# Spreading the right-hand attention scores through a row in DRAM instead of by TensorE transposes

## The chip, the core and the metric

The kernel runs on one core of a Trainium2 chip. The time is the device time of one execution in microseconds (us). The core's engines work side by side, each through its own instructions in order: TensorE (PE, its weight loads shown apart as PEld), VectorE (DVE), ScalarE (ACT), GpSimd (POOL) and SyncE (SP), which issues the transfers between DRAM and the on-chip memory. An instruction waits for what it needs by semaphores. Matrix products land in eight PSUM banks; everything else is in SBUF, whose 128 partitions are the rows of each tile.

## What is computed

64 graphs of 256 nodes with 256 features, float32, and a 0/1 adjacency matrix for each. Two layers, each after a layer norm and a relu, each added to its input: a gated graph network of three rounds, then one graph attention layer.

```python
def _L0_gnn_ref(x, adj, weight, w_ih, w_hh, b_ih, b_hh):
    A = (adj != 0).astype(x.dtype)
    h = x
    for i in range(3):
        m = jnp.einsum('bnd,de->bne', h, weight[i])
        aggr = jnp.einsum('bst,bsd->btd', A, m)
        h = _gru_cell(aggr, h, w_ih, w_hh, b_ih, b_hh)
    return h

def _L1_gnn_ref(x, adj_matrix, W, a):
    h = jnp.einsum('bnd,od->bno', x, W)
    a_left, a_right = (a[0, :D], a[0, D:])
    e = (h @ a_left)[:, :, None] + (h @ a_right)[:, None, :]
    e = jnp.where(e > 0, e, 0.2 * e)
    e = jnp.where(adj_matrix == 0, -1e9, e)
    alpha = jax.nn.softmax(e, axis=-1)
    return jnp.einsum('bij,bjd->bid', alpha, h)

h = jnp.maximum(_layernorm(x), 0.0)
x = x + _L0_gnn_ref(h, adj, ...)
h = jnp.maximum(_layernorm(x), 0.0)
return x + _L1_gnn_ref(h, adj, ...)
```

The change concerns one line of the attention layer: in `e`, row i holds the left score of node i, one number for each partition, plus the right scores of all 256 nodes, which every partition needs along its row.

## The kernel before

The graphs go in 32 pairs of two (graph 0 and graph 1 of a pair). For each pair the kernel runs the layer norm ("in"), three rounds of the gated network, and the attention. The network's products are made of float32 values split into parts (`split`), so that a gate is a group of matmuls 512 wide: "top" groups (L456), a scaling of the bank on ACT ("scale", L470), then a "rest" group (L461). The letters are the gates: r, z, nh (the hidden side of n), ni (its input side), each for two halves of the features (r 0, r 1, ...). "prop" (L541) multiplies by the adjacency matrix, "turn" and "back" (L523, L584) transpose between the two layouts.

The attention of a pair, per graph g:

- "mid g": layer norm and relu of the residual (statistics on DVE, a power on POOL, relu on ACT at L496).
- "dot g" (L606): four products on DVE with the folded vectors W·a_left and W·a_right, each summed along the row into one column of a small tile: columns 12 and 13 are the left scores of the two halves of the nodes, 14 and 15 the right scores.
- "right g" (L617): two TensorE transposes, each with the column broadcast over 128 columns as the stationary operand, give a PSUM bank in which every partition holds all 256 right scores.
- "leaky g" (L621): two ACT passes read that bank, add the left score as the bias and apply the leaky relu.
- "mask g" (L624), "max g" (L626) on DVE, then "exps" on ACT (L633) for both graphs at once, with the load of another function table ahead of it.
- "p turn" (L648, PE), "p copy" (L652, ACT), "mix" (L657, PE), "mix copy" (L661, ACT), "project" (L666, PE), "out" (L671, DVE) and the store (L674, SP).

Nothing is issued in the order in which it is written. Every operation is an `Op` with an engine, a time in which it occupies the engine (`occ`), a time until its result is there (`lat`), and the buffers that it reads and writes. `Plan.run` then lays all of them out once, over the whole program: at each step it takes the operation that can start earliest, and among equals the one with the lowest priority number, which is worked back from due times and moved by the table `LEAD` ("right 0" is put back by 15000 ns there). Up to four pairs are open at once, so that between the steps of one pair's attention stand the gates of the next pair and the first steps of the one after it. The order so found is the order of the instructions on each engine; on the chip an engine keeps to it, also where an instruction has to wait. The result of an operation on the same engine counts as available after `occ`, on another engine after `lat`:

```python
for q in o.preds:
    t = max(t, q.start + q.occ if q.eng == e else q.end)
```

Buffers come from classes with a fixed number of slots: 28 "full" and 32 "round" tiles of 128 x 512 in SBUF, 12 "small" ones, and 8 "bank" tiles in PSUM. `pe`, `act`, `dve`, `pool` and `dma` make operations of the engine in their name.

Of the kernel before, what the change touches and what calls it, by code (L numbers as in the profile page):

```python
# [10 lines left out]
F32 = mybir.dt.float32  # L11
# [181 lines left out]
def tile_gated_gnn_then_gat(  # L193
# [35 lines left out]
    nc = tc.nc  # L229
    P = 128  # L230
    B, N, D = x.shape
    L = weight.shape[0]
    NB = N // P
# [5 lines left out]
    NPAIR = B // G  # L239
# [5 lines left out]
    plan = Plan(WINDOW, LEAD)  # L245
# [2 lines left out]
    plan.slot_class("x", [const.tile([P, GN], F32, name=f"x{i}") for i in range(2)])  # L248
    plan.slot_class("adj", [const.tile([P, GN], I32, name=f"adj{i}") for i in range(2)])
    plan.slot_class("small", [const.tile([P, 32], F32, name=f"small{i}") for i in range(12)])  # L250
    plan.slot_class("bank", [psum.tile([P, GN], F32, name=f"bank{i}") for i in range(8)])

    ALL = (0, 1)
    ONE = (0,)

    def parts(b):
        return b.t[:, :GN].rearrange("p (k d) -> p k d", k=2)
# [3 lines left out]
    def pe(name, n, fn, **kw):  # L261
        return plan.op(name, "PE", n, n + 220, fn, **kw)

    def act(name, n, fn, **kw):
        plan.op(name, "ACT", n, n + 170, fn, **kw)

    def dve(name, n, fn, **kw):
        plan.op(name, "DVE", n, n + 160, fn, **kw)

    def dve2(name, n, fn, **kw):  # L270
        plan.op(name, "DVE", n, n + 160, fn, port=True, **kw)

    def pool(name, n, fn, **kw):
        plan.op(name, "POOL", n, n + 200, fn, port=True, **kw)
# [5 lines left out]
    MM, TR, PROP, PASS = 432, 109, 120, 232  # L280
# [6 lines left out]
    ident = const.tile([P, P], F32, name="ident")  # L287
# [187 lines left out]
    def norm_relu(name, src, dst):  # L475

        sm = Buf("small")
        st = lambda k: sm.t[:, 6 * k : 6 * k + 6]
        mv = lambda: sm.t[:, 12:16].rearrange("p (k s) -> p k s", s=2)

        def stats():
            for nb in range(NB):
                nc.vector.bn_stats(st(nb), parts(src)[:, nb, :])
            for nb in range(NB):
                nc.vector.bn_aggr(mv()[:, nb, :], st(nb))

        dve(name + " stats", 900, stats, r=[(src, ALL)], w=[(sm, (0, 1))])
        dve(name + " eps", 70, lambda: nc.vector.tensor_scalar(sm.t[:, 16:18], mv()[:, :, 1], LN_EPS, None, op0=ALU.add),  # L488
            r=[(sm, (0, 1))], w=[(sm, (2,))])
        pool(name + " pow", 900, lambda: nc.gpsimd.tensor_tensor(sm.t[:, 16:18], sm.t[:, 16:18], nhalf, ALU.pow),  # L490
             r=[("nhalf", ONE)], w=[(sm, (2,))])
        dve2(name + " shift", 70, lambda: nc.vector.scalar_tensor_tensor(sm.t[:, 18:20], mv()[:, :, 0], -1.0, sm.t[:, 16:18],
                                                       op0=ALU.mult, op1=ALU.mult),
            r=[(sm, (0, 1, 2))], w=[(sm, (3,))])
        for nb in range(NB):
            act(name + " relu", 495, lambda nb=nb: nc.scalar.activation(  # L496
                parts(dst)[:, nb, :], parts(src)[:, nb, :], AF.Relu,
                bias=sm.t[:, 18 + nb : 19 + nb], scale=sm.t[:, 16 + nb : 17 + nb]),
                r=[(src, (nb,)), (sm, (2, 3))], w=[(dst, (nb,))])

    def pair(p):
# [7 lines left out]
        for g in range(G):  # L509
            dve2("A", 340, lambda g=g: nc.vector.tensor_scalar(A[g].t, ADJ[p][g].t, 0.0, None, op0=ALU.not_equal),  # L510
                r=[(ADJ[p][g], ALL)], w=[(A[g], ONE)])
# [3 lines left out]
                r=[(h[g], ALL), (hi[g], ONE)], w=[(lo[g], ONE)])  # L515
# [13 lines left out]
        for i in range(L):  # L529
# [22 lines left out]
            for db in range(DB):  # L552
# [4 lines left out]
                    r=[(pr, ONE), ("b_rz", ONE)], w=[(r_, ONE)])  # L557
# [3 lines left out]
                    r=[(ph, ONE), (r_, ONE)], w=[(u, ONE)])  # L561
# [3 lines left out]
                    r=[("vec", ONE)], w=[(u, ONE)])  # L565
# [3 lines left out]
                    r=[(pz, ONE), ("b_rz", ONE)], w=[(z_, ONE)])  # L569
# [8 lines left out]
            for g in range(G):  # L578
# [11 lines left out]
                else:  # L590
                    act(f"hi {g}", A512 + 10, lambda b=hi[g], pt=pt: nc.scalar.copy(b.t, pt.t), r=[(pt, ONE)], w=[(hi[g], ONE)])
                    dve(f"lo {g}", V512, lambda b=hi[g], c=lo[g], pt=pt: nc.vector.tensor_sub(c.t, pt.t, b.t.bitcast(F32)),  # L592
                        r=[(pt, ONE), (hi[g], ONE)], w=[(lo[g], ONE)])
# [5 lines left out]
        for g in range(G):  # L599
            pool("fill", 520, lambda b=pm_[g]: nc.gpsimd.memset(b.t, NEG_INF), w=[(pm_[g], ALL)])  # L600
            norm_relu(f"mid {g}", XR[g], hb[g])
            sm = sms[g]
            for nb in range(NB):
                for n in range(2):
                    c = 12 + n * NB + nb
                    dve2(f"dot {g}", 425, lambda g=g, nb=nb, n=n, c=c, sm=sm: nc.vector.scalar_tensor_tensor(  # L606
                        parts(sc[g])[:, nb, :], parts(hb[g])[:, nb, :], 1.0, va[:, n, :], op0=ALU.mult, op1=ALU.mult,
                        accum_out=sm.t[:, c : c + 1]),
                        r=[(hb[g], (nb,)), ("va", ONE)], w=[(sm, (c,)), (sc[g], (nb,))])


            pR = Buf("bank")

            def right(sm=sm, pR=pR):
                for nb in range(NB):
                    c = 12 + NB + nb
                    nc.tensor.transpose(pR.t[:, ts(nb, P)], sm.t[:, c : c + 1].to_broadcast([P, P]), ident)  # L617

            pe(f"right {g}", 2 * TR, right, r=[(sm, (14, 15))], w=[(pR, ONE)])
            for nb in range(NB):  # L620
                act(f"leaky {g}", 365, lambda b=sc[g], nb=nb, pR=pR, sm=sm: nc.scalar.activation(  # L621
                    parts(b)[:, nb, :], pR.t[:, :N], AF.Prelu, bias=sm.t[:, 12 + nb : 13 + nb], alpha=LEAKY_SLOPE),
                    r=[(pR, ONE), (sm, (12 + nb,))], w=[(sc[g], (nb,))])
            dve2(f"mask {g}", 660, lambda g=g: nc.vector.copy_predicated(pm_[g].t, A[g].t.bitcast(I32), sc[g].t),  # L624
                r=[(A[g], ONE), (sc[g], ALL)], w=[(pm_[g], ALL)])
            dve(f"max {g}", 610, lambda b=pm_[g], sm=sm: nc.vector.tensor_reduce(sm.t[:, 0:NB], parts(b), AX.X, ALU.max, negate=True),  # L626
                r=[(pm_[g], ALL)], w=[(sm, ONE)])

        def exps():
            for g in range(G):  # L630
# [6 lines left out]
                w=[(b, ALL) for b in pm_] + [(s, (1,)) for s in sms])  # L637

        for g in range(G):
            sm = sms[g]  # L640
            dve("recip", 70, lambda sm=sm: nc.vector.reciprocal(sm.t[:, 8 : 8 + NB], sm.t[:, 4 : 4 + NB]),
                r=[(sm, (1,))], w=[(sm, (2,))])
# [35 lines left out]
    for p in range(NPAIR):  # L678
        if p > 0:
            plan.pair = p  # L680
            load_pair(p)
        pair(p)
# [28 lines left out]
```

## Time and profile before

| | |
|---|---|
| median of 3 runs | 2248.85 us (2248.42 to 2250.21) |
| profiled execution, time | 2247.52 us |
| profiled execution, span from first to last instruction | 2245.7 us |
| PE busy in the stretch 115 to 1100 us | 982.58 of 985 us |
| "right", L617 matmul records | 128, mean 279 ns |
| "leaky", L621 | 128, mean 472 ns |
| DRAM traffic | 71.75 MB, mean 32 GB/s, all queues |

The profile is one execution, recorded instruction by instruction. A group of instructions has a count, a busy time and a mean length; records of matmuls overlap, since TensorE begins one before the last has left, so the time that a matmul takes from the engine is read from one start to the next. The waits name, for an engine and a line, the instruction that ended an idle time. The chain of waits goes back from the last instruction to what released it. The answer on a tile's transfers gives the time from a transfer's issue to its landing.

### The profile page before, as it was taken

To read this page: it belongs to the slowest core of one execution; us is meant where nothing else is said; L and a number is where in the kernel's file an instruction comes from. 1 tells how busy PE (TensorE), PEld (TensorE's weight loads), DVE (VectorE), ACT (ScalarE), POOL (GpSimd) and SP (SyncE) were. 2 spreads that over 40 slices of the span, in tenths; PEclk is the share of its full clock that TensorE was granted. 3 is DMA by queue.
4 is the path that set the end of the run, shared out by engine and by line. 5 is a ranking of instruction groups with operands and counts; after the bars stand their busy time and mean duration, and the time that the engine had idled before them with its cause. 6 is when DMAs were issued, how large, how long until landed. Compare 5 with 4: busy or idle time off the path is not lost.

```text
span 2245.7 us, 31163 instructions
## 1 busy us (share of the span) xinstructions
PE 2213.2 (99%) x10977; PEld 1822.5 (81%) x10977; DVE 1825.2 (81%) x4084; ACT 1662.8 (74%) x3069; POOL 140.6 (6%) x198
## 2 busy tenths in 40 slices
PE   8999999999999999999999999999999999999997
PEld 6788888888888888888888888888888888888875
DVE  7878877879878888778788778797787887787974
ACT  8677777777777777777777777777777777777764
POOL 1000000000000000000000000000000000000000
PEclk9999999999999999999999999999999999999998
DMA  3000111001111001110011110011110011100000
GB/s 103 20 20 29 38 38 38 20 20 38 38 39 34 24 20 38 38 38 29 15 33 39 38 38 20 20 39 38 38 34 24 20 38 38 38 29 15 15 19 28
DMA packets 72541, 71.75 MB, mean 32 GB/s; under 512 B 4272, under 2 KB 72384, under 8 KB 72384
## 3 DMA queue, kind: packets, MB, share of 16 engines
q1 hardware_dynamic: 72352, 69.75, 10.2%
q8 instruction: 86, 1.41, 0.3%
q14 instruction: 71, 0.58, 0.1%
q10 hardware_dynamic: 32, 0.01, 0.0%
HBM read 52.96 MB, written 16.78 MB: 31 GB/s over the span
## 4 chain that ended last, share of the span: by engine, by line
PE 70%; DVE 19%; ACT 8%; issue 3%; DMA 0%; ACTq 0%; POOL 0%; DVEq 0%; POOLq 0%
PE bank L456 32%; PE bank L461 16%; PE bank L541 5%; PE bank L657 5%; PE bank L666 5%; DVE round L442 4%; PE bank L584 3%; DVE round L443 3%; ACT full L496 2%; DVE full L314 2%; DVE full L574 2%; DVE full L573 2%; ACT bank L470 2%; DVE round L592 2%; PE bank L648 1%
## 5 line engine op out<-in xcount | busy, mean ns | idle before, releaser
L456 PE MATMUL bank<-round,fac_hh 128*128 128x512 f32 x2304 | 635.0, 402 | 0.5 <-DVE round L442 0.5
L456 PE MATMUL bank<-round,fac 128*128 128x512 f32 x2304 | 600.3, 395 | 0.0
L456 PEld LDWEIGHTS bank<-round,fac 128*128 128x128 f32 x2304 | 433.2, 188 | 103.4
L456 PEld LDWEIGHTS bank<-round,fac_hh 128*128 128x128 f32 x2304 | 410.7, 189 | 74.3 <-DVE round L442 1.0
L461 PE MATMUL bank<-round,fac_hh 128*128 128x512 f32 x1152 | 383.0, 413 | 0.7 <-ACT bank L470 0.7
L470 ACT ACTIVATE bank<-bank 128x512 f32<-128x512 f32 x576 | 327.5, 579 | 62.5 <-PE bank L456 62.3
L461 PE MATMUL bank<-round,fac 128*128 128x512 f32 x1152 | 355.5, 398 | 1.0 <-ACT bank L470 1.0
L441 ACT CAST round<-full 128x512 fp32r<-128x512 f32 x384 | 238.3, 621 | 156.9 <-DVE full L314 156.9
L442 DVE TENSOR_TENSOR round<-full,full 128x512 fp32r<-128x512 f32 x384 | 259.5, 689 | 8.7
L573 DVE TENSOR_TENSOR full<-full,full 128x512 f32<-128x512 f32 x192 | 129.3, 686 | 168.6 <-ACT full L567 168.5
L461 PEld LDWEIGHTS bank<-round,fac 128*128 128x128 f32 x1152 | 210.2, 188 | 61.9 <-ACT bank L470 16.4
L443 DVE SCALAR_TENSOR_TENSOR round<-round,full 128x512 fp32r<-128x512 f32 x384 | 255.5, 686 | 3.4
L461 PEld LDWEIGHTS bank<-round,fac_hh 128*128 128x128 f32 x1152 | 202.0, 189 | 48.5 <-ACT bank L470 16.4
L541 PEld LDWEIGHTS bank<-round,round 128*128 128x128 f32 x1536 | 204.7, 189 | 14.2 <-DVE round L592 0.9
L541 PE MATMUL bank<-round,round 128*128 128x256 f32 x1536 | 214.9, 285 | 0.7 <-DVE round L592 0.7
L572 DVE TENSOR_TENSOR full<-full,full 128x512 f32<-128x512 f32 x192 | 128.3, 681 | 106.4 <-ACT full L564 106.4
L490 POOL TENSOR_TENSOR small<-small,nhalf 128x2 f32<-128x2 f32 x128 | 106.1, 829 | 1477.6 <-DVE small L488 1476.8
L567 ACT ACTIVATE full<-bank,b_rz 128x512 f32<-128x512 f32 x192 | 132.2, 689 | 71.4 <-PE bank L461 71.1
L545 ACT COPY full<-bank 128x512 f32<-128x512 f32 x192 | 112.9, 588 | 88.2 <-PE bank L541 88.2
L314 DVE TENSOR_SCALAR full<-full 128x512 int32<-128x512 int32 (+1 forms) x400 | 161.7, 418 | 6.5 <-ACT full L545 5.0
L563 DVE TENSOR_TENSOR full<-full,bank 128x512 f32<-128x512 f32 x192 | 131.9, 687 | 40.8 <-PE bank L461 31.4
L556 ACT ACTIVATE full<-bank,b_rz 128x512 f32<-128x512 f32 x192 | 131.2, 684 | 40.4 <-PE bank L461 40.1
(74 smaller groups left out, 2723.0 us busy)
## 6 DMA issues: line engine op xcount, KB each, us to landing
x<-in_x_dram SPq DMA_DIRECT2D x64, 256.0 KB, 2.7
adj<-in_adj_dram SPq DMA_DIRECT2D x64, 256.0 KB, 2.7
full<-in_x_dram SPq DMA_DIRECT2D x64, 256.0 KB, 3.1
out_dram<-full SPq DMA_DIRECT2D x64, 256.0 KB, 2.2
full<-in_L_gnn_w_ih_dram SPq DMA_DIRECT2D x3, 256.0 KB, 4.2
full<-in_L_gnn_weight_dram SPq DMA_DIRECT2D x3, 256.0 KB, 4.6
full<-in_L_gnn_w_hh_dram SPq DMA_DIRECT2D x3, 256.0 KB, 5.3
full<-in_L_gnn_W_dram SPq DMA_DIRECT2D x1, 256.0 KB
```

The costliest lines, as they stand in the source:

```text
L314: dve2(name, 60 + n * 0.54, lambda: nc.vector.tensor_scalar(dst().bitcast(I32), src().bitcast(I32), CUT, None, op0=ALU.bitwise_and), r=r, w=w)
L441: act(name + " 0", C512, lambda: nc.scalar.copy(v0.t, t.t), r=[(t, ONE)], w=[(v0, ONE)])
L442: dve2(name + " 1", V512, lambda: nc.vector.tensor_sub(v1.t, v.t, t.t), r=[(v, ALL), (t, ONE)], w=[(v1, ONE)])
L443: dve2(name + " d", V512, lambda: nc.vector.scalar_tensor_tensor(vd.t, v1.t.bitcast(F32), -SPLIT, t.t, op0=ALU.mult, op1=ALU.add), r=[(v1, ...
L456: nc.tensor.matmul(bank.t, f(m, j, kb), b.t, start=(first and n == 0), stop=True, skip_group_check=True)
L461: nc.tensor.matmul(bank.t, f(m, 2, kb), s[kb][2].t, start=False, stop=True, skip_group_check=True)
L470: act(name + " scale", A512, lambda: nc.scalar.activation(bank.t, bank.t, AF.Identity, bias=bias, scale=1.0 + C), r=[("vec", ONE)], w=[(ba ...
L541: nc.tensor.matmul(pa.t[:, ts(g, N)], parts(b)[:, sb, ts(db, P)], parts(A[g])[:, sb, :], start=(n == 0), stop=(n == len(terms) - 1))
L556: act(f"r {db}", 575, lambda b=r_, k=pr, db=db: nc.scalar.activation(b.t, k.t, AF.Sigmoid, bias=b_rz[:, db : db + 1]), r=[(pr, ONE), ("b_r ...
L563: dve(f"u add {db}", V512, lambda u=u, k=pn: nc.vector.tensor_add(u.t, u.t, k.t), r=[(pn, ONE)], w=[(u, ONE)])
L567: act(f"z {db}", 575, lambda b=z_, k=pz, db=db: nc.scalar.activation(b.t, k.t, AF.Sigmoid, bias=b_rz[:, DB + db : DB + db + 1]), r=[(pz, O ...
L573: dve2(f"d mul {db}", V512, lambda d=d, b=z_: nc.vector.tensor_mul(d.t, d.t, b.t), r=[(z_, ONE)], w=[(d, ALL)])
```

## The change

For all pairs but the last, the two transposes of "right" are replaced by two transfers on SP. "line" writes the two columns of right scores (128 partitions x 2 numbers of 4 bytes) into a row of 256 numbers in DRAM. "right" reads this row back with all 128 partitions as its destination, 1 KB into each, into a "full" tile. "leaky" reads that tile in place of the PSUM bank. There are four rows in DRAM for this, and their slots are handed out by the planner like those of the other classes. The last pair keeps the transposes. The planner's table `LEAD` and all other operations are as they were; the planner lays out the whole order anew.

```diff
+    dram = ctx.enter_context(tc.tile_pool(name="dram", bufs=1, space=bass.MemoryType.DRAM))
+    plan.slot_class("line", [dram.tile([1, N], F32, name=f"line{i}") for i in range(4)])
     plan.slot_class("bank", [psum.tile([P, GN], F32, name=f"bank{i}") for i in range(8)])
...
-            pR = Buf("bank")
-
-            def right(sm=sm, pR=pR):
-                for nb in range(NB):
-                    c = 12 + NB + nb
-                    nc.tensor.transpose(pR.t[:, ts(nb, P)], sm.t[:, c : c + 1].to_broadcast([P, P]), ident)
-
-            pe(f"right {g}", 2 * TR, right, r=[(sm, (14, 15))], w=[(pR, ONE)])
+            if p < NPAIR - 1:
+                line, pR = Buf("line"), Buf("full")
+                plan.op(f"line {g}", "SP", 150, 2800, lambda line=line, sm=sm: nc.sync.dma_start(
+                    line.t.rearrange("o (nb q) -> (o q) nb", q=P), sm.t[:, 12 + NB : 12 + 2 * NB]),
+                    r=[(sm, (14, 15))], w=[(line, ONE)])
+                plan.op(f"right {g}", "SP", 150, 2600, lambda line=line, pR=pR: nc.sync.dma_start(
+                    pR.t[:, :N], line.t.to_broadcast([P, N])), r=[(line, ONE)], w=[(pR, ONE)])
+            else:
+                pR = Buf("bank")
+
+                def right(sm=sm, pR=pR):
+                    for nb in range(NB):
+                        c = 12 + NB + nb
+                        nc.tensor.transpose(pR.t[:, ts(nb, P)], sm.t[:, c : c + 1].to_broadcast([P, P]), ident)
+
+                pe(f"right {g}", 2 * TR, right, r=[(sm, (14, 15))], w=[(pR, ONE)])
             for nb in range(NB):
                 act(f"leaky {g}", 365, lambda b=sc[g], nb=nb, pR=pR, sm=sm: nc.scalar.activation(
                     parts(b)[:, nb, :], pR.t[:, :N], AF.Prelu, bias=sm.t[:, 12 + nb : 13 + nb], alpha=LEAKY_SLOPE),
```

## The prediction

> **What bounds the kernel now.** I read the head of the page and its chain, then the busy time by stretches, then the waits, then the groups of the removed operation and the timelines around it, last the answers on the transfers.
>
> ```profile
> span 2245.7 us, 31163 instructions
> PE 2213.2 (99%) x10977; PEld 1822.5 (81%) x10977; DVE 1825.2 (81%) x4084; ACT 1662.8 (74%) x3069; POOL 140.6 (6%) x198
> ...
> PE 70%; DVE 19%; ACT 8%; issue 3%; DMA 0%; ACTq 0%; POOL 0%; DVEq 0%; POOLq 0%
> ```
>
> ```profile
> 1100.00:2150.00 1050.00, 1047.82 (x5237) 867.44 (x5236) 860.76 (x1921) 785.91 (x1447) 64.89 (x88) 1.00 0.10 31
> 2150.00:2245.70 95.70, 76.37 (x346) 60.44 (x344) 58.16 (x138) 52.97 (x99) 2.76 (x4) 0.91 0.05 17
> ```
>
> TensorE is the bound and is full: in the 1050 us of the first stretch it is idle for 2.2. (Columns: window, length, busy PE, PEld, DVE, ACT, POOL, clock, DMA share, GB/s.) So a slot taken from PE's queue shortens the run by that slot, and a wait put in front of PE lengthens it by the wait: there is nothing to absorb it. The waits show how little the operation costs now:
>
> ```profile
> ACT full L652 <- PE bank L648: 29.7, 33, 1.0
> ...
> PE bank L648 <- ACT full L633: 3.0, 1, 3.0
> ...
> ACT full L621 <- PE bank L617: 2.9, 11, 0.9
> ```
>
> ACT's leaky pass (L621) hardly waits for the transposes (L617), and PE waits for the exponentials (L633) only in the last pair. The removed transposes and their slot, on PE's timeline in a middle pair (start, length):
>
> ```profile
> 813.22 1.09 PE L456 MATMUL bank<-round,fac 128*128 128x512 f32 x4
> 814.15 0.62 PE L461 MATMUL bank<-round,fac 128*128 128x512 f32 x2
> 814.61 0.38 PE L617 MATMUL bank<-ident,small 128*128 128x128 f32 x2
> 814.83 0.60 PE L523 MATMUL bank<-ident,full 128*128 128x128 f32 x4
> ...
> 829.70 0.38 PE L617 MATMUL bank<-ident,small 128*128 128x128 f32 x2
> 829.84 1.18 PE L456 MATMUL bank<-round,fac_hh 128*128 128x512 f32 x4
> 830.85 1.10 PE L456 MATMUL bank<-round,fac 128*128 128x512 f32 x4
> ```
>
> A record lasts 0.27 us or more, but records overlap; start to next start counts. The first pair of transposes holds PE for 0.22. The second holds it for 0.14, and the four matmuls behind it take 1.01 instead of the usual 0.93: 0.22 as well.
>
> **What the Trainium skill says.** "DMA: Bandwidth & Descriptors", section "Anatomy of one DMA", puts about 2 us of fixed cost on a transfer, most of it the receipt from the written memory. The trace agrees: a 256 KB store lands 2.2 us after its issue, a 256 KB load of x after 2.7. The same page, "Rules for kernel authors", says that a non-contiguous last dimension becomes one descriptor per element, and that a DMA that reads what another wrote has to wait for the other's completion. No run here shows the first yet. By it the column becomes 256 pieces of 4 bytes, and by the second the two latencies add. "TensorE: Matmul & The Clock Gate", table at the top, calls the queues of ScalarE and VectorE strict FIFOs: an ACT instruction that waits holds all behind it. The waits and timelines agree.
>
> **The change, part by part.**
> *Removed.* 31 pairs x 2 graphs = 62 couples of transposes, 62 x 0.22 = 13.6 us of PE. Nothing else falls away. The bank that they filled comes free, but PE's 2.2 idle us in the stretch above leave nothing for a further bank to win.
>
> *Added on the queues.* 62 writes and 62 broadcast reads on SP. SP's loads of the next pair stand ahead of them, the stores of this pair follow some 20 us later, so nothing urgent is behind them. Traffic grows by 62 x 128 KB = 8 MB on 71.75, at a DMA share of 0.10. Both at nothing; if the queues were crowded the two latencies below would grow.
>
> *The new wait.* Leaky now needs two transfers in series after the last dot product.
>
> ```profile
> L674 SPq DMA_DIRECT2D out_dram<-full x64: 383/384/387, 164.5 to 2242.6; - x64
> ...
> DMA to landing us min/median/max: 2.1/2.2/4.6
> ```
>
> The answer for x is 2.5/2.7/4.6. Write: a 256 KB store is 256 packets of 1 KB, the column 256 pieces of 4 bytes, so I take the store's 2.2. Queue 1 of the page gives a packet 10.2% x 16 x 2245.7 / 72352 = 51 ns, so the store's 16 packets per engine are 0.8 of that. If a small piece cost nothing the write would take 1.4; if a piece under 512 B cost twice a packet (the page's table of specifications speaks of read-modify-write there; no trace here shows it) 3.0. Read: x's 2.7 less half its packets, 8 x 51 ns = 0.4, gives 2.3. Low bound 2.1, as no load here lands sooner; high 3.1, if 128 reads of one row get in each other's way. Hand-offs: DVE to SP 0.03 (846.37 + 0.87 against SP's issue at 847.27), and 0.05 to 0.1 for each of the other two. Sum 4.7, from 3.7 to 6.3.
>
> *What covers it.* The planner gives its ops on one engine a start after the other's issue, not after its landing; so to it "right" starts 150 ns after "line", and it puts leaky about 2.75 us behind the dot products. I take the cover from the order in which the changed kernel issues its work, with durations of the trace of before. Zero is the issue of r 1's rest on PE. PE then has 2 + 1 + 2 + 4 + 1 couples of wide matmuls (r 1 rest, nh 1 rest, ni 1 top, z 0 top, ni 1 rest) at 0.93 for two couples: 4.66. The turn of the next pair adds 0.60 (L523 above), ACT copies it (0.47 to its next instruction): leaky of graph 1 has its turn at 5.8. Against that the last dot product: r 0's sigmoid starts 0.2 to 0.5 after zero (two relu passes stand ahead), 0.69; DVE's multiply 0.60, dot product 0.43: 1.9 to 2.2, and I take 2.4 for the other dot products in DVE's queue. Cover 5.8 - 2.4 = 3.4. ACT waits 4.7 - 3.4 = 1.3. Graph 0's row is fetched meanwhile and comes as its leaky has its turn, so it adds nothing.
>
> *Who waits behind it.* On ACT, from the first leaky to the exponentials, in the new order, by the spacings of ACT's timeline: leaky 2 x 0.37, tanh 0.61, three copies or scales of a bank in 0.47 to 0.52 (prop 1, prop 0, z 1's scale) and nh 0's scale 0.52, sigmoid 0.58, leaky 2 x 0.37, three casts (h0, g0, g1) 0.53: 6.3. Exponentials 3.4 with their table load (833.02 to 836.40), hand-off 0.1: 9.8. PE from the same moment: what it still has ahead of the turn of the exponentials, counted from zero, is 4.66 + 0.44 (turn) + 2 x 0.96 (prop) + z 0 rest 0.93 + z 1 top 1.86 + six groups of four (nh 0 top, r 1, z 1 rest, r 0 twice, ni 0) 5.58 = 15.4, less 5.8: 9.6. So the new order holds no slack there (the old one put the turn 0.6 after the exponentials' end, 836.40 to 836.97): even without ACT's wait PE would be 0.15 late. With it, PE stands 1.3 + 0.15 = 1.45 per pair, a good half of it already at nh 0's top, which needs h0's cast from ACT. DVE is held too (mask 1 needs leaky) but nothing of it reaches PE sooner.
>
> *Sum.* 31 x 1.45 = 45, less 13.6: +31 us. Profiled execution: span 2245.7, time 2247.52; 2247.5 + 31 = 2279. The median shown is 1.3 above that execution: 2280. The last pair keeps its transposes; the tail is costed at nothing, 2 us either way.
>
> **Rivals.**
> *A. The small pieces are dear.* Write 3.0, read 3.1, L = 6.3: wait per pair 6.3 - 3.4 + 0.15 = 3.05; 94.6 - 13.6 = +81, 2330. For it: the page counts 4272 packets under 512 B but prices none of them, so nothing here shows what a 4-byte write costs. Against: 256 pieces are only 16 per engine.
> *B. The cover holds, and the change is faster.* Place: leaky of graph 1 on ACT. It decides at a round trip of 3.4 - 0.15 + 13.6 / 31 = 3.7 us; at 3.2 or less the whole slot is won, 2248.85 - 13.6 = 2235. For it: ACT is idle for 26% and ahead of PE elsewhere (it waits 82.4 us for L456 in all). Against: 3.7 is my low bound for two latencies in series.
> *C. Wait and slot cancel,* within 4.5 us: a round trip of 3.6 to 3.8, or DVE's dot products done half a us earlier together with a cheap write. 2249.
>
> **How the numbers follow.** Forecast 0.70 (round trip 4.0 to 5.6, wait 0.75 to 2.3: +10 to +58, 2259 to 2307); A 0.17; B 0.08; C 0.05. About 0.2% is what a measurement of this kernel can tell from no change. Most of B is faster: 0.06; same 0.05; slower 0.89. The range reaches from the cheap end of the forecast, 2256, into the first half of A, 2322.
>
> **What would show it.** In the changed profile: L617's transposes at 4 (now 128); a new wait of ACT's leaky for the landed row, 31 times or more, 1 to 1.6 us each; new waits of PE for ACT's cast and for the exponentials, 1.45 us per pair, and PE at 97% (2200 of 2277); landings of about 2.2 and 2.3. Wrong if leaky finds its row landed (B), if the two landings add to more than 5.5 (A), or if PE stands at another line, which would mean that the new order, not the transfers, costs the time.

## The result, and the profile after

The changed kernel takes 2806.07 us in the median of 4 runs (2803.83 to 2813.82), the kernel before 2249.24 beside it: a ratio of 1.2482, 95% interval 1.2456 to 1.2507. The direction was as forecast, the size was not: +557 us against +31.

The page of the changed kernel: span, busy times, and the two new transfers (KB each, median us from issue to landing).

```profile
span 2805.9 us, 30945 instructions
...
PE 2312.1 (82%) x10853; PEld 1886.9 (67%) x10853; DVE 1832.8 (65%) x4084; ACT 1677.4 (60%) x3069; POOL 136.8 (5%) x198
...
full<-line SPq DMA_DIRECT2D x62, 128.0 KB, 4.8
line<-small SPq DMA_DIRECT2D x62, 1.0 KB, 9.1
```

PE has lost its fill: idle for 2805.9 - 2312.1 = 493.8 us against 32.5 before, which is +461. And it is busy for 98.9 us more although 124 matmuls are gone. The two make up the whole difference of the spans, 560. The write of the column, the smallest transfer of the kernel (1 KB), takes the longest to land.

Its waits (engine and line, what it waited for: us in total, times, longest):

```profile
ACT full L632 <- DMA full<-line: 527.5, 62, 15.6
DVE full L635 <- ACT full L632: 512.4, 61, 15.3
...
PE bank L458 <- ACT round L443: 297.9, 30, 15.2
...
PE bank L463 <- ACT bank L472: 159.1, 38, 13.0
...
PE bank L659 <- ACT full L644: 3.0, 1, 3.0
```

Most of the links are the predicted ones: leaky (now L632) waits for the row, DVE's mask for leaky, PE for the cast (L443) that stands behind leaky on ACT. PE's second wait is for a scale of a bank (L472) that stands behind the other graph's leaky, and not for the exponentials (L644), as predicted: for these PE waits once, 3.0 us, as before. And ACT waits at both graphs, 62 times, and 8.5 us each. The timeline of one pair, first SP, then ACT, then PE (start, length, in brackets the idle time before):

```profile
995.28 0.37 SPq L617 DMA_DIRECT2D line<-small  x1
1003.55 0.34 SPq L620 DMA_DIRECT2D full<-line  x1
1003.99 0.39 SPq L617 DMA_DIRECT2D line<-small  x1
1014.97 0.33 SPq L620 DMA_DIRECT2D full<-line  x1
```

```profile
998.00 0.59 ACT L529 COPY full<-bank 128x512 f32<-128x512 f32 x1 [0.31 <-PE bank L525]
1008.62 0.51 ACT L632 ACTIVATE full<-full,small 128x256 f32<-128x256 f32 x1 [10.04 <-DMA full<-line]
...
1019.78 0.91 ACT L632 ACTIVATE full<-full,small 128x256 f32<-128x256 f32 x2 [7.58 <-DMA full<-line]
```

```profile
1001.56 1.10 PE L458 MATMUL bank<-round,fac 128*128 128x512 f32 x4
1012.25 3.78 PE L458 MATMUL bank<-round,fac_hh 128*128 128x512 f32 x8 [9.59 <-ACT round L443]
1021.73 1.22 PE L463 MATMUL bank<-round,fac_hh 128*128 128x512 f32 x2 [5.70 <-ACT bank L472]
```

Graph 1's column is written for 8.2 us before SP can issue the read. The last dot product of graph 0 ended at 998.59, but its write is issued at 1003.99: it stands behind that read in SP's queue, and the read behind the landing. So the two round trips run one after the other. After the first wait PE's eight matmuls take 3.78 us. A like group of eight took 2.02 before:

```profile
819.96 2.02 PE L456 MATMUL bank<-round,fac_hh 128*128 128x512 f32 x8
```

Where the write's time goes shows when the same pair is cut into stretches, here the busy share of the 16 DMA engines in 40 slices of 0.25 us between 995 and 1005 and the packets in it:

```profile
DMA  0000230000000000000000000000000000000000
...
DMA packets 272, 0.00 MB, mean 0 GB/s; under 512 B 272, under 2 KB 272, under 8 KB 272
```

and the stretches themselves (window, length, busy PE, PEld, DVE, ACT, POOL with counts, granted clock, DMA share, GB/s):

```profile
997.00:1003.00 6.00, 5.66 (x35) 4.64 (x33) 3.33 (x10) 1.28 (x3) 0.00 (x0) 1.00 0.00 0
1003.00:1005.00 2.00, 0.00 (x0) 0.00 (x0) 0.00 (x0) 0.00 (x0) 0.00 (x0) 0.95 0.00 0
1005.00:1007.00 2.00, 0.00 (x0) 0.00 (x0) 0.00 (x0) 0.00 (x0) 0.00 (x0) 0.50 0.06 23
1012.25:1016.03 3.78, 3.78 (x8) 2.47 (x8) 0.82 (x2) 0.00 (x0) 0.00 (x0) 0.50 0.17 1
```

The pieces are sent within 0.5 us, from 996.0 to 996.5. For the next 7 us no packet moves, and the write has still not landed. So the cost is no work of the DMA engines; it lies between the last packet and the landing. The Trainium skill ("DMA: Bandwidth & Descriptors", section "Anatomy of one DMA") says that the receipt of the target memory is most of a DMA's fixed cost of about 2 us; the section is written for transfers that GpSimd issues, and these are issued by SP. The place agrees; the size here, 8.2 us for this write, is four times that. The 272 packets are the 256 pieces of the forecast and 16 more. The last two stretches show the second loss: with PE idle its granted clock falls to 0.50, and it is still 0.50 during the eight matmuls after the wait. Over the whole run it is 0.898 against 0.996.

Landings of the writes come in two sizes. A pair's first write (graph 1) takes 8.2 us in the median, its second (graph 0), issued just behind the read of the first, 10.4. In this pair the second write is issued at 1003.99, but its packets move only between 1007 and 1008.5, among and after those of the read, which had itself been late.

### The profile page after: what moved, and what is told of

The parts are those of the page before. It is cut to its first block, busy times and chain, and to the rows that moved or that the text cites. A ratio compares the mean times of both kernels' runs of the same rounds, so it can differ in the third digit from the quotient of the medians.

```text
span 2805.9 us, 30945 instructions
## 1 busy us (share of the span) xinstructions
PE 2312.1 (82%) x10853; PEld 1886.9 (67%) x10853; DVE 1832.8 (65%) x4084; ACT 1677.4 (60%) x3069; POOL 136.8 (5%) x198
## 5 line engine op out<-in xcount | busy, mean ns | idle before, releaser
L458 PE MATMUL bank<-round,fac_hh 128*128 128x512 f32 x2304 | 698.7, 434 | 298.5 <-ACT round L443 297.9
L458 PEld LDWEIGHTS bank<-round,fac_hh 128*128 128x128 f32 x2304 | 461.8, 209 | 405.4 <-ACT round L443 311.2
L458 PE MATMUL bank<-round,fac 128*128 128x512 f32 x2304 | 617.6, 402 | 0.0
L463 PE MATMUL bank<-round,fac_hh 128*128 128x512 f32 x1152 | 397.4, 427 | 156.6 <-ACT bank L472 156.6
L458 PEld LDWEIGHTS bank<-round,fac 128*128 128x128 f32 x2304 | 443.0, 193 | 104.6
L472 ACT ACTIVATE bank<-bank 128x512 f32<-128x512 f32 x576 | 332.7, 583 | 126.5 <-PE bank L458 123.8
L635 DVE COPY_PREDICATED full<-round,full 128x512 f32<-128x512 int32 x64 | 46.7, 730 | 512.5 <-ACT full L632 512.4
L632 ACT ACTIVATE full<-full,small 128x256 f32<-128x256 f32 x124 | 59.4, 503 | 527.5 <-DMA full<-line 527.5
L463 PE MATMUL bank<-round,fac 128*128 128x512 f32 x1152 | 372.6, 410 | 2.5 <-ACT bank L472 2.5
L463 PEld LDWEIGHTS bank<-round,fac_hh 128*128 128x128 f32 x1152 | 206.0, 195 | 213.7 <-ACT bank L472 184.8
L443 ACT CAST round<-full 128x512 fp32r<-128x512 f32 x384 | 234.5, 620 | 109.9 <-DVE full L316 109.9
L463 PEld LDWEIGHTS bank<-round,fac 128*128 128x128 f32 x1152 | 221.3, 195 | 60.2 <-ACT bank L472 11.5
L575 DVE TENSOR_TENSOR full<-full,full 128x512 f32<-128x512 f32 x192 | 132.3, 689 | 136.4 <-ACT full L569 136.3
L566 ACT ACTIVATE full<-full,vec 128x512 f32<-128x512 f32 x192 | 138.9, 723 | 98.0 <-DVE full L565 94.2
L492 POOL TENSOR_TENSOR small<-small,nhalf 128x2 f32<-128x2 f32 x128 | 97.0, 758 | 1626.5 <-DVE small L490 1530.4
L594 DVE TENSOR_TENSOR round<-bank,round 128x512 fp32r<-128x512 f32 x128 | 87.9, 688 | 117.7 <-ACT round L593 115.5
```

What stands on the lines that cost most here:

```text
L443: act(name + " 0", C512, lambda: nc.scalar.copy(v0.t, t.t), r=[(t, ONE)], w=[(v0, ONE)])
L458: nc.tensor.matmul(bank.t, f(m, j, kb), b.t, start=(first and n == 0), stop=True, skip_group_check=True)
L463: nc.tensor.matmul(bank.t, f(m, 2, kb), s[kb][2].t, start=False, stop=True, skip_group_check=True)
L472: act(name + " scale", A512, lambda: nc.scalar.activation(bank.t, bank.t, AF.Identity, bias=bias, scale=1.0 + C), r=[("vec", ONE)], w=[(ba ...
L566: act(f"tanh {db}", 615, lambda u=u, en=en: nc.scalar.activation(u.t, u.t, AF.Tanh, bias=b_i[:, en : en + 1]), r=[("vec", ONE)], w=[(u, ONE)])
L575: dve2(f"d mul {db}", V512, lambda d=d, b=z_: nc.vector.tensor_mul(d.t, d.t, b.t), r=[(z_, ONE)], w=[(d, ALL)])
```

## The experiments

Theory 1: the loss is the wait for the round trip, and nothing else. Its first rival, theory 2: the new order or the small writes' traffic costs by itself. Inside theory 1 it was open what makes a write of 1 KB take 9.1 us: a cost of each piece (1a), a fixed one (1b), or pieces that meet at one place in DRAM (1c). Times are medians; those without an interval are of a single run. Before stood at 2248.0 to 2248.6 in these runs.

### The wait taken away: no_wait and own_tile

```diff
-                    parts(b)[:, nb, :], pR.t[:, :N], AF.Prelu, bias=...
+                    parts(b)[:, nb, :], va[:, 1, :], AF.Prelu, bias=...
```

> Leaky reads a constant tile (va) of the same size in place of the fetched row; both transfers are still issued, nothing on ACT waits for them, and the issue order is that of the changed kernel. Left out: the right scores in leaky. Theory 1 (the whole loss is the wait for the round trip): before less the removed slots, plus the 0.15 us per pair by which the new order alone is late: 2249 - 13.6 + 4.6 = 2240, between 2233 and 2250; PE idle under 40 us, clock near 0.996. Theory 2 (the new issue order or the traffic of small writes costs by itself): above 2300.

Measured: 2502.05 us, ratio 1.1134 (1.1115 to 1.1153). By the number alone this is theory 2. The waits tell another story:

```profile
DVE full L316 <- DMA full<-line: 192.4, 30, 10.7
...
ACT full L663 <- DMA full<-line: 87.3, 25, 4.9
```

The fetched tile is handed out again once leaky is done, as the planner sees it. With leaky no longer waiting, the next users of that tile wait for the landing instead. The experiment had moved the wait, not removed it. So once more, with leaky reading the constant as before and a tile of its own for the row:

```diff
+    sink = [const.tile([P, N], F32, name=f"sink{i}") for i in range(1)]
-                    pR.t[:, :N], line.t.to_broadcast([P, N])), r=[(line, ONE)], w=[(pR, ONE)])
+                    sink[k], line.t.to_broadcast([P, N])), r=[(line, ONE)], w=[(pR, ONE)])
```

> As in no_wait, leaky reads a constant tile, but now the fetched row also goes to a tile of its own that nothing reads and no other operation reuses, so that no engine but SP can wait for a transfer. Left out: the right scores. Theory 1 (the loss is waits for the transfers, in no_wait by the operations that reuse the tile as a buffer): 2233 to 2250, no wait of ACT, DVE or PE for a transfer of the row. Theory 2 (order or traffic): above 2300.

Measured: 2245.65 us, ratio 0.9987 (0.9981 to 0.9994), with the write still landing after 9.4 us and the read after 4.6, and no wait for either outside SP. The waits of PE that are left:

```profile
PE bank L464 <- ACT bank L473: 9.2, 34, 1.1
PE bank L587 <- DVE full L577: 8.6, 17, 3.9
```

Theory 2 falls: the new order, the issues and the traffic together cost no more than the removed transposes save. This run is also about the most that the change can win in this order: 2.6 us.

### What makes the write slow: one_piece, pieces_8_bytes, one_column, pitch_512, pitch_64, pieces_16_bytes

One contiguous piece in place of 256:

```diff
-                    line.t.rearrange("o (nb q) -> (o q) nb", q=P), sm.t[:, 12 + NB : 12 + 2 * NB]),
+                    line.t, b.t[0:1, :N]),
```

> The write takes one contiguous row of 1 KB of one partition of the dot products' scratch tile, after the dot products, in place of 256 pieces of 4 bytes; the read-back waits for it as in the changed kernel. Left out: the right scores. Theory 1a (the 9.1 us of the write are 256 small pieces, 16 on each engine): it lands in 1.5 to 2.2 us, the read stays at 4.3 to 4.8, round trip 6.2 to 7.2 against a cover of 3.4, so PE waits 2.9 to 3.9 per pair: 2249 - 14 + 31 x 3.4 = 2340, 2320 to 2365. Theory 1b (a write of a row in DRAM that is read back has a long fixed cost): it lands above 6 us and the time stays above 2550.

Measured: 2246.68 us. Its SP timeline in one pair:

```profile
810.07 0.25 SPq L617 DMA_DIRECT2D line<-full  x1
811.25 0.34 SPq L620 DMA_DIRECT2D full<-line  x1
```

The read follows 1.18 us after the write's issue and lands after 2.8. Both transfers are quicker than expected, and the experiment helps itself besides: the piece taken needs only the first two dot products, so the write starts 0.9 us earlier than the real column could (810.07 against the last one's end at 810.99). So no wait is left to see, and the time says nothing of the real column. 1b falls by the landing: a row in DRAM that is read back at once has no long fixed cost.

Pieces of 8 bytes, the row laid out node by node:

```diff
-                    line.t.rearrange("o (nb q) -> (o q) nb", q=P), sm.t[:, 12 + NB : 12 + 2 * NB]),
+                    line.t.rearrange("o (q nb) -> (o q) nb", q=P), sm.t[:, 12 + NB : 12 + 2 * NB]),
```

> The row is laid out node by node, so that the two neighbouring numbers of a partition go out as one piece of 8 bytes: 128 pieces in place of 256; leaky reads the row with a stride. Nothing else changes. Theory 1a (cost per piece, (9.1 - 1.4) / 16 = 0.48 us for each of the 16 pieces of an engine): 8 pieces take 3.9, landing 5.3 us; the round trip falls by 3.8 for each graph, two in series, so the time by up to 31 x 7.6 = 236 us: 2560 to 2640. If the cost is per 4 bytes or fixed: 9.1 us and 2800.

Measured: 2451.3 us, write 3.8 us, both less than 1a allows for half the pieces (2560 and 5.3). So it is not the number alone. Two runs part number and place. One column only (128 pieces of 4 bytes, as dense as before), and all 256 pieces, each 512 bytes from the next:

```diff
+                    line.t[:, :P].rearrange("o (nb q) -> (o q) nb", q=P), sm.t[:, 12 + NB : 13 + NB]),
```

> Only one of the two columns is written: 128 pieces of 4 bytes side by side (the other half of the row is filled once at the start). Left out: the right scores of the second half of the nodes. If the number of pieces sets the landing, it is that of 128 pieces of 8 bytes, 3.8 us, and the time that of that run, about 2450. If what counts is how many pieces of other engines share a block of DRAM (16 of them in 64 bytes here, 8 with pieces of 8 bytes), it stays well above: 5 to 9 us.

```diff
+    plan.slot_class("line", [dram.tile([1, N * P], F32, name=f"line{i}") for i in range(4)])
...
+                    line.t.rearrange("o (nb q k) -> (o q) nb k", q=P, k=P)[:, :, 0], sm.t[:, 12 + NB : 12 + 2 * NB]),
```

> The 256 pieces of 4 bytes go to addresses 512 bytes apart in DRAM instead of side by side; the read takes the first 1 KB of that area. Left out: all but two of the right scores (the rest of the row is filled once at the start). Theory 1a (a cost of each small piece on its engine): the write still lands at 8 to 10 us. Theory 1c (pieces of different engines meet in one block of DRAM and queue up there): it lands at 1.5 to 3 us, the read at about 2.8, and the time falls to 2250 to 2330.

Half the pieces, equally dense: 9.1 us and 2759.87. All the pieces, far apart: 1.6 us and 2295.29. 1a falls and 1c holds, as far as it says that neighbouring pieces are slow; whether they have to come from different DMA engines, as was expected, was not tried. The last two runs of this set change the density, the second one the size of the pieces and of the read as well:

```diff
+                    line.t.rearrange("o (nb q k) -> (o q) nb k", q=P, k=16)[:, :, 0], sm.t[:, 12 + NB : 12 + 2 * NB]),
```

> 256 pieces of 4 bytes at addresses 64 bytes apart, one in each 64 bytes. Left out: all but 16 of the right scores. If pieces only meet within 64 bytes, the write lands at 1.6 us as with 512 bytes between them and the time is 2295. If they meet in blocks of 512 bytes (8 of them here), it lands at about 3.8 and the time is 2400 to 2450.

```diff
+                    line.t.rearrange("o (q c) -> (o q) c", q=P), sm.t[:, 12:16]),
+                    pR.t, line.t.to_broadcast([P, 2 * N])), r=[(line, ONE)], w=[(pR, ONE)])
```

> The 16-byte pieces in the issue order of the changed kernel. Write 2.0 to 2.6, read 3.0 to 3.6 (256 KB), hand-offs 0.2: round trip 5.2 to 6.4 against the cover of 3.4, so a wait of 1.9 to 3.1 per pair with the 0.1 of the order: 2246 + 31 x 2.5 = 2323, 2300 to 2345.

| run | pieces | pieces in 64 bytes | write to landing, min/median/max us | first / second write of a pair, median us | read, median us | time, us |
|---|---|---|---|---|---|---|
| changed kernel | 256 x 4 B | 16 | 7.7/9.1/11.3 | 8.2 / 10.4 | 4.8 | 2806 |
| one_column | 128 x 4 B | 16 | 7.4/9.1/10.4 | 8.1 / 9.7 | 4.6 | 2760 |
| pieces_8_bytes | 128 x 8 B | 8 | 2.7/3.8/5.7 | 2.9 / 4.9 | 4.2 | 2451 |
| pieces_16_bytes | 128 x 16 B | 4 | 1.4/2.2/4.0 | 1.4 / 2.6 | 3.7 (256 KB) | 2360 |
| pitch_64 | 256 x 4 B | 1 | 1.5/1.6/3.1 | 1.6 / 1.6 | 2.9 | 2295 |
| pitch_512 | 256 x 4 B | 1 | 1.5/1.6/3.1 | 1.6 / 1.6 | 2.9 | 2295 |

(The traces have the read's landing for 14 to 17 of the 62 reads of a run, all of them second reads of a pair.) At one size of piece, 4 bytes, the landing depends on how densely the pieces lie and not on their number. The rows of 8 and 16 bytes lie between in density, but there the pieces are also larger. Nor is the landing in proportion to the density: the first writes of pieces_16_bytes land as early as single pieces, and the 2.2 of that run, which seemed to meet the expectation, is a mixture with second writes that stand behind a read. Its time is above what was expected. As 64 bytes apart is as good as 512, the place where the pieces meet is 64 bytes or smaller. What the memory does there no run shows. Nor is it settled why the read, too, is slower just after a dense write: in the changed kernel its first packets move 3 us after its issue (1003.55 to about 1006.5), in pitch_64 after 1 us. (In the two pitch runs the read takes the first 1 KB of the area, in which only 16 or 2 of the pieces lie.)

pitch_64 is also the kernel for which the prediction had been made: small pieces that cost no more than a store. One pair of it, SP and then ACT:

```profile
826.79 0.37 SPq L619 DMA_DIRECT2D line<-small  x1
828.76 0.34 SPq L622 DMA_DIRECT2D full<-line  x1
830.17 0.36 SPq L619 DMA_DIRECT2D line<-small  x1
831.92 0.33 SPq L622 DMA_DIRECT2D full<-line  x1
```

```profile
831.70 0.51 ACT L634 ACTIVATE full<-full,small 128x256 f32<-128x256 f32 x1 [1.56 <-DMA full<-line]
...
835.15 0.92 ACT L634 ACTIVATE full<-full,small 128x256 f32<-128x256 f32 x2
```

From the write's issue to leaky are 4.91 us; ACT had come to leaky at 831.70 - 1.56 = 830.14, 3.35 us after that issue. Graph 0's write goes out at 830.17, as its dot products end, and its leaky doesn't wait. What PE waits for:

```profile
PE bank L460 <- ACT round L445: 29.0, 30, 1.5
PE bank L465 <- ACT bank L474: 16.6, 37, 1.1
...
PE bank L661 <- ACT full L646: 3.0, 1, 3.0
```

### The planner told the truth: known_latency, landed, landed_8_bytes, landed_16_bytes

```diff
-                plan.op(f"line {g}", "SP", 150, 2800, lambda line=line, sm=sm: nc.sync.dma_start(
+                plan.op(f"line {g}", "SP", 9200, 9300, lambda line=line, sm=sm: nc.sync.dma_start(
-                plan.op(f"right {g}", "SP", 150, 2600, lambda line=line, pR=pR: nc.sync.dma_start(
+                plan.op(f"right {g}", "SP", 350, 4900, lambda line=line, pR=pR: nc.sync.dma_start(
```

> Only the planner's numbers change: the write occupies SP for 9200 ns with 9300 until landing, the read 350 and 4900, in place of 150/2800 and 150/2600, so that leaky is placed some 20 us after the dot products. Theory 1 (loss is a latency that the order doesn't cover): the wait goes, and what is left is before less the removed slots, 2235 to 2250. Theory 3 (slow writes cost something besides latency, or the later leaky finds no room in the four open pairs): above 2300.

Measured: 2306.29 us, ratio 1.0256 (1.0241 to 1.0272). The write still takes 7.8 us (the trace has only the landings of first writes, which took 8.2 in the changed kernel), and ACT never waits for the row. 500 of the 557 us are gone by numbers of the planner alone. Most of what is left over before, 58 us, is in other waits of PE: its idle time is 2306.0 - 2227.0 = 79 us against 32.5, 30.2 of it for a cast, 13.7 for a scale on ACT and 11.9 for DVE; PE's busy time is 13.8 us longer. So the number is that of theory 3. Which of its two causes it is, this run doesn't separate.

```diff
+                plan.op(f"line {g}", "SP", 380, 8200, lambda line=line, sm=sm: nc.sync.dma_start(
+                plan.op(f"landed {g}", "landed", 0, 0, lambda: None, r=[(line, ONE)], w=[(line, ONE)])
+                plan.op(f"right {g}", "SP", 340, 3600, lambda line=line, pR=pR: nc.sync.dma_start(
```

> The planner's numbers again (write 8200 to its landing, read 3600), but with SP free after the issue and the read placed after the landing by an operation of no length between them, so that leaky of graph 1 stands 12 us behind its dot products and no load is displaced. The transfers are those of the changed kernel. Theory 1 (a latency that is covered costs nothing): 2232 to 2255. Theory 3 (an order with a later leaky has waits of its own, as in known_latency): 2270 to 2330.

Measured: 2399.35 us, ratio 1.0655 (1.062 to 1.069), above both theories. ACT waits for the row again, 31 times, in one graph of each pair, and the read's landings have become long:

```profile
ACT full L633 <- DMA full<-line: 150.3, 31, 7.8
```

```profile
L621 SPq DMA_DIRECT2D full<-line x62: 332/332/640, 138.9 to 2340.3; - x62
...
DMA to landing us min/median/max: 3.7/5.9/9.8
```

In this order graph 0's write is in flight when graph 1's read is issued, right at the landing of its own row: these first reads take 6.4 us in the median, the second ones, with no write beside them, 4.5. With pieces that meet less, in the same order (the edit of landed with that of pieces_8_bytes, then with that of pieces_16_bytes):

> The order of landed with the pieces of pieces_8_bytes (128 of 8 bytes, write 3.8 us). Theory 1 (what landed still lost was a read that stood beside the other graph's slow write, 5.9 us and up to 9.8, longer than its cover): the row is there in time, no wait of ACT for it, and the time is that of an order without such waits, 2235 to 2260. Theory 3 (the order itself waits): above 2280 with no wait for a transfer.

> The same order, with all four numbers of a partition (left and right scores) as one piece: 128 pieces of 16 bytes, a row of 2 KB and a read of 256 KB; leaky reads the right scores from it with a stride. If the landing follows the number of pieces in 64 bytes of DRAM (16: 9.1 us, 8: 3.8, alone: 1.6), with 4 it is 2.0 to 2.6. Time as landed_8_bytes or up to 5 us less.

Measured: 2261.44 us, ratio 1.0058 (1.0042 to 1.0075), and 2262.11, ratio 1.0061 (1.0046 to 1.0076). Writes of 3.0 and 1.4 us, reads of 3.1 and 3.3; ACT waits for the row for 1.5 us in all in the first and 0.5 in the second. The write of 1.4 is quicker than expected (2.0 to 2.6): only first writes have a landing in this trace, and they took 1.4 in pieces_16_bytes too. That the dense writes slowed the read is so supported. A dense write beside a read is not enough for it, though: in known_latency graph 1's reads, issued some 3.5 us after their own row had landed and some 7 us after the issue of the other graph's dense write, took 3.0 in the median. What delays the read stays open. Both kernels still take 13 us more than before, and landed_8_bytes is 1.4 us above its expected range. In the two stretches from 115 to 2150 us PE is idle for 16.6 and 16.8 us, against 11.4 in own_tile and 4.6 before. Over the whole span PE is busy for 11 to 12 us more than in own_tile with as many matmuls; why was not followed further. No kernel with the right scores in it beats the one with the transposes.

## Why the prediction was right in most of its waits and wrong in its size

- *Removed slots, 13.6 us.* own_tile has 9.7 us less of PE busy than before. The new order takes back most of it: PE's idle time between 115 and 2150 us rises by 6.8, or 0.22 per pair, where 0.15 was taken.
- *Cover 3.4 us.* 3.35 in the pair of pitch_64 shown.
- *Round trip 4.7 us, wait 1.45 per pair.* Where the write is as quick as a store (pitch_64), the round trip is 4.91, and the wait costs (2294.8 - 2245.65) / 31 = 1.59 per pair over own_tile, where the sum has 1.3; 2295 in place of 2280. To this point the size of the sum stands.
- *"And for the exponentials."* This place was wrong. PE waits for h0's cast as forecast (29.0 us in 30 waits in pitch_64, "a good half" of 1.45 per pair), but for the exponentials only once, 3.0 us. In place of that wait there is one for a scale (16.6 us) and 9.0 us more of PE busy than in own_tile; that the total comes so near the forecast is luck in this part. The prediction let PE's turn wait for all four exponentials of a pair. In the pair of pitch_64 the turn (L661) starts before the last of them (L646) has ended:

```profile
840.96 0.49 ACT L646 ACTIVATE full<-full,small 128x256 f32<-128x256 f32 x1
841.00 1.16 PE L661 MATMUL bank<-ident,full 128*128 128x128 f32 x8
```

- *The step that failed: the write, "I take the store's 2.2", from 1.4 to 3.0.* It measured 9.1. The bounds were made of packets: 16 on each engine, free or at twice their price. The packets are indeed gone in 0.5 us, and small size alone costs little: the same 256 pieces land after 1.6 when they lie apart. The cost comes after the last packet and appears where small pieces lie side by side in DRAM; a store of packets of 1 KB, the nearest row, doesn't show it. The upper end was thus no bound. The prediction's sign for this, two landings that add to more than 5.5, came true with 9.1 + 4.8 = 13.9.
- *"Graph 0's row is fetched meanwhile and comes as its leaky has its turn, so it adds nothing."* True while a write lands before the next dot products end (pitch_64). With 8 us and more it failed through the same term: SP waits for the landing with graph 0's write queued behind. "Nothing urgent is behind them" had looked at the loads and stores and missed the other graph's pair of transfers. Both graphs then waited, 10.04 and 7.58 us in the pair shown.
- *The read, 2.3 within 2.1 to 3.1.* 2.8 to 2.9 in one_piece and the pitch runs, 4.8 just after a dense write.
- *Not in the sum: the clock.* The spans of the changed kernel and of pitch_64 lie 2805.9 - 2293.0 = 512.9 us apart. PE's idle time gives 493.8 - 80.5 = 413.3 of it, by the three points above; the other 99.6 are PE's longer busy time. The clock accounts for it: 238 us of PE's busy time lie in stretches granted 0.50, 11 in pitch_64, and half of the difference is an estimated 113.
- *Rivals.* A had the place, the small pieces, but priced them at 6.3 us for the round trip; in the pair shown it is 995.28 to 1008.62, 13.3. B's condition, a row that is there in time, came about in one_piece, by its head start, and in orders that lose elsewhere; even there the whole slot is not won, 2247 and not 2235. The forecast's cheap end is 2259, not the 2256 that the range starts from.

## What to carry to other kernels

Price a small write by one with the same layout in memory and not by its packets: a transfer has a time after its last packet, and neighbouring small pieces may land five times later than the same pieces spread out (8.2 us against 1.6). Where a transfer waits for another's landing, all that is queued behind it waits too, so a planner has to be told the landing, or its order leaves no room where the time is needed. And taking a wait away where buffers are handed out can move it to the buffer's next user: look there before drawing a conclusion.

## What the runs showed of the hardware

- 128 or 256 pieces of 4 bytes, written side by side into DRAM, land after 8.1 to 8.2 us in the median with no other transfer of the pair in flight, and after 9.7 to 10.4 behind a read; 64 or 512 bytes apart after 1.6. In the pair shown the pieces were sent within 0.5 us.
- One piece of 1 KB lets the dependent read go 1.18 us after its issue, quicker than the 2.1 to 2.2 of a 256 KB store.
- A 128 KB read issued right at the landing of a dense write takes 4.5 to 4.8 us in the median, with another dense write just begun 6.4 and up to 9.8; some 3.5 us after the landing it takes 3.0, and in the runs without dense writes 2.8 to 2.9.
- The granted clock of PE fell to 0.50 in gaps of some 10 us and was still there just after one, when eight matmuls took 3.78 us, against 2.02 for a like group before.
